# A four-layer convolution network on one core: input loads mixed with transposes, averages next to dense slots, halo copies spread out, the last halves turned sooner, and one quarter's squares paced by VectorE's sums

## The chip, the core and the metric

The kernel runs on one core of one Trainium2 chip, in one launch. The metric is the device time in microseconds; smaller is better. The engines are called TensorE (PE in the profile, its weight loads PEld), VectorE (DVE), ScalarE (ACT), GpSimd (POOL) and SyncE (SP, which here only issues DMAs). GB/s and KB are as the profile prints them.

## What is computed

The input x has the shape (1024, 16, 16, 16): batch, height, width, channel, all float32. Four layers follow each other, each adding its result to x:

```python
x = x + L0(_gn(x))   # a tensor-train matrix: three small cores, together 4096 x 4096
x = x + L1(_gn(x))   # two fixed 3x3 filters by channel, fc0 (48 -> 128), relu, fc1 (128 -> 16), masks
x = x + L2(_gn(x))   # a 3x3 convolution, 16 -> 16 channels, plus bias
x = x + L3(_gn(x))   # as L1, with weights of its own

def _gn(v, G=8, eps=1e-5):          # normalise over height, width and two channels
    g = v.reshape(B, H, W, G, C // G)
    m, s = mean(g, (1, 2, 4)), var(g, (1, 2, 4))
    return ((g - m) / sqrt(s + eps)).reshape(v.shape)
```

In L1 and L3 the sum x + d is multiplied by a mask: a place is kept where the largest of the 3 x 3 neighbours (over height and width) of channel 3 is above 0.1, in the layer's input and in d. The kernel counts the neighbours that are above it by small matmuls (pcnt). fc0 reads rows of 48 consecutive numbers of the array with its 48 channels ahead of width and height.

## The kernel before

**Tiling.** The batch is cut into two chunks of 512 columns (n = 0 and 1). A chunk of x is a tile X0 or X1 in the on-chip memory: 128 partitions, 32 lines, 512 columns. Between layers x goes through DRAM (`xf`). All matmuls are float32; each stands in the trace as two instructions.

**Stages.** The program is one sequence of stages: the first layer in five phases (up to about 1760 us), L1 on chunk 0 and on chunk 1 (to about 2270), the convolution on chunk 0 and on chunk 1 (to about 2490), L3 on chunk 0 (to about 2740) and on chunk 1 with the output (to the end). While a stage multiplies, the group norm of the next one runs beside it: VectorE sums lines (`line_sum`), TensorE averages the sums over groups by a matmul with `gm_cw` or `gm_wc` (`mean`, `mean_q`), ScalarE copies the average out (`held`), VectorE subtracts it (`each`), ScalarE or VectorE squares (`squares`), VectorE sums the squares, TensorE averages those (`var`, `var_q`), `rstd` makes the root's inverse, and VectorE scales. In `parts_cw` this goes by four quarters of eight lines.

**Order.** Every engine runs its instructions in the order in which the program writes them. `run` writes it: it goes through the stage's own steps (`main`), and after each it appends those steps of the background list whose due time, worked out from costs and a part (lo to hi) of the stage, has passed. Numbers in the background lists are pauses or costs, not waits of the machine.

```python
for i, step in enumerate(main):
    step()
    ...
    while todo and (todo[0][0] < part or i == len(main) - 1):
        todo.pop(0)[1]()
```

**First layer.** At the start chunk 0 is read by SyncE, turned by TensorE transposes (`turn`, line 866) and stored as lines in `xr` by POOL (line 881). Chunk 1 is read by POOL in eight loads of 1024 KB (line 848) during phase 0. SyncE reads `gq` (line 1040), from which `build` makes weights on TensorE (pw, line 1057); `build` takes the four banks of the tag "w", and ScalarE copies them out (line 1062). Transposes and the small matmuls `pg` of `gs` take banks by the tag "mw", which alternates between the one bank of tag "m" and the four of tag "w" (`bank`, with `either`).

**L1 and L3.** A slot is either a group of up to four matmuls of 32 rows by 128 columns each, in different row strips of the array (ph, line 1521), or a dense slot: four matmuls of 128 rows by 32 columns in different column strips (fc1, po, line 1358). `plan` gives their order; between two dense slots stand one to five ph slots, three in most places. ScalarE takes ph to hid with a relu (line 1524), VectorE takes po to u (line 1370), and GpSimd, or VectorE for the last tiles, applies mask and residual. The dense result and all averages share two banks of tag "o" (`shared[0]` is "o" in these stages, "m" in the others). Ready rows of ph have six banks. `after(n, fn)` writes fn n slots later. In the last stage the last four quads are cut into halves of 256 columns, and `turn` transposes a finished residual (ptx, line 1420) to the output's layout; with the last tile of a half, four stores of 1024 KB go out on SyncE (line 1435).

**Convolution.** Rows of output come in pairs, in seven steps: `first`, `middle` for each row, one `across`, and `last` for each; `across` takes rows of neighbours from a halo tile `hx` that ScalarE copies (line 1210), eight copies for every four rows, one popped from `pending` after each step. ScalarE also takes the results out (line 1270).

Of the kernel before, what the change touches and what calls it, by code (L numbers as in the profile page):

```python
# [103 lines left out]
def conv_preact_kernel(ctx: ExitStack, tc: tile.TileContext, a: dict, out: bass.AP):  # L104
# [585 lines left out]
    def rstd(st, rows=slice(0, P)):  # L690
# [16 lines left out]
        return [2, root, 3, (6, newton)]  # L707

    def norm_lines(X, on_act=True):
        parts = [lambda l=l: X[:, l : l + 2] for l in range(0, NL, 2)]  # L710
        s1, steps = line_sum(parts, "s1", False)
        s2, more = line_sum(squares(X, 0, NL, on_act), "s2", True, not on_act)
        st = {}

        def mean():
            st["p"] = psum([P, NB], "pmean")
            T.matmul(st["p"], gm_wc, s1["s"], start=True, stop=True)

        def var():
            st["v"] = psum([P, NB], "pvar")  # L720
            T.matmul(st["v"], gm_wc, s2["s"], start=True, stop=True)

        def keep():
            st["ve"] = work([P, NB], "n", "ve")
            V.tensor_scalar(st["ve"], st["v"], GN_EPS, None, ALU.add)

        subs = each(X, 0, NL, lambda: st["m", 0], ALU.subtract)
        steps = steps + [5, mean, 2, held(st), 2] + centred(subs, more)
        steps += [5, var, 2, keep] + rstd(st)
        return steps + by_rows(each(X, 0, NL, lambda: st["r"], ALU.mult))  # L730

    def parts_cw(X, on_act):

        st = {}
        N = defaultdict(list)
        for q in range(4):
# [4 lines left out]
            N["sums"].append(more1)  # L741
            N["sq"].append(
                centred(each(X, l0, 8, lambda q=q: st["m", q], ALU.subtract), more2)
            )
            rows = slice(32 * q, 32 * q + 32)

            def mean_q(s1=s1):
                st["p"] = psum([P, NB], "pmean")
                T.matmul(st["p"], gm_cw, s1["s"], start=True, stop=True)  # L749

# [15 lines left out]

            N["mean"].append(mean_q)
            N["var"].append(var_q)
            N["keep"].append(keep_q)
# [12 lines left out]
    def norm_cw(X, on_act):  # L782
# [6 lines left out]
        for q in (1, 2):  # L789
            steps += woven(  # L790
                sums[q + 1], (1, var[q - 1]), (3, keep[q - 1]), (3, mean[q]), (4, hold[q])
            ) + [2] + sq[q][:4]
# [233 lines left out]
    def layer_train():  # L1026
# [18 lines left out]
        def build(u):  # L1045
# [6 lines left out]
            k0 = 2 if m1 == 2 else 0  # L1052
            pw = [bank([P, 2, 16 - 4 * k0, S], "w", "pw") for _ in range(4)]
            for v in range(2):
                for r in range(4):
# [134 lines left out]
    def layer_conv(X, n, other):  # L1190
# [64 lines left out]
        def step(*fs):  # L1255
            def go():
                for f in fs:
                    f()
                if pending:
                    pending.pop(0)()  # L1260
# [24 lines left out]
    def layer_nca(X, n, l, L, xo=None):  # L1285
# [119 lines left out]
        def residual(q, w2, hf=None):  # L1405
# [7 lines left out]
            else:  # L1413
                after(8, lambda: turn(q, w2, r, hf))

# [65 lines left out]
        def step(slot):  # L1481
            def go():
# [4 lines left out]
                else:  # L1487
                    for x in slot:
                        tile_of_row(*x)
                due = [fn for n, fn in later if n <= t]  # L1490
                later[:] = [x for x in later if x[0] > t]
# [42 lines left out]
    def run(layer, us, loads, *spans, by=0.0):  # L1534
# [21 lines left out]
        for i, step in enumerate(main):  # L1556
            step()
            part = (i + 1) / len(main)
            while done < len(loads) and done < len(loads) * part / (by or 1e-9):
                loads[done]()  # L1560
                done += 1
            while todo and (todo[0][0] < part or i == len(main) - 1):
                todo.pop(0)[1]()

# [22 lines left out]
    with ExitStack() as es:  # L1587
# [32 lines left out]
            x for j in range(2) for i in range(4) for x in stat[j][i] + lines[j][4 * i : 4 * i + 4]  # L1620
        ]
        run(
            steps_of(phases[0]), 130, (),
            (late[:6] + loads[0:4] + late[6:] + loads[4:] + later + woven_in + tail + normed(0, 1) + combined(0, False), 0.0, 1.0),
        )
# [4 lines left out]
        for i in (2, 3):  # L1630
# [3 lines left out]
            )  # L1634
        nst, N = parts_cw(X0, True)
        for q in range(4):
# [23 lines left out]
    with ExitStack() as es:  # L1660
# [7 lines left out]
        run(  # L1668
            (lambda: None, main1), 108, load_cw(X0, xf[3][0]) + [put(L3)], (norm_cw(X0, True), 0.09, 1.06), by=0.07
        )  # L1670
# [37 lines left out]
```

## Time and profile before

| | us |
|---|---|
| median of three runs | 3043.31 (3041.16 to 3043.62) |
| the profiled execution | 3039.35 |
| its span in the trace | 3037.6 |

| engine | what it does most | busy us |
|---|---|---|
| TensorE | po of the first layer (line 1134), 3584 instructions | 1573.9 |
| TensorE | ph of L1 and L3 (line 1521), its two largest groups | 568.8 and 298.6 |
| ScalarE | hid (line 1524), 1040 instructions of 680 ns | 656.2 |
| VectorE | r (line 1170), 576 instructions of 684 ns | 377.9 |
| GpSimd | res and u (lines 1410, 1409), 123 each | 205.4 and 192.9 |

Such a table is read with care: busy time is a mean over stages that have different limits. The profile also gives the span in 40 slices, with the share of full speed that TensorE's clock was granted, and the trace answers for any stretch which engine was busy and which wait ended before an instruction. A wait is named after the instruction that came last by the profile, for instance "PE ph L1521 <- ACT hid L1524": a matmul of line 1521 waited for ScalarE's instruction of line 1524.

### The profile page before, as it was taken

What the parts mean: (1) busy time and instruction counts of PE and PEld (TensorE: products, weight loads), DVE (VectorE), ACT (ScalarE), POOL (GpSimd) and SP (SyncE); (2) the same over time, 40 slices, a digit from 0 to 9 for tenths busy, and PEclk for the clock granted to TensorE, in tenths of its full rate; (3) what the DMA queues carried; (4) which work ended last, traced back from release to release, by engine and by line L of the source; (5) the groups of instructions that cost most, each with busy time, mean ns of one, the idle gap of its engine ahead of it and who ended that gap; (6) DMA issues with size and microseconds to landing.
All of it is one profiled execution on the core that took longest, in us unless ns stands there. A gap on an engine that the chain in (4) does not pass through costs nothing.

```text
span 3037.6 us, 36802 instructions
## 1 busy us (share of the span) xinstructions
PE 2973.1 (98%) x13810; PEld 1245.4 (41%) x13810; DVE 1764.0 (58%) x2352; ACT 1102.7 (36%) x1822; POOL 669.9 (22%) x727
## 2 busy tenths in 40 slices
PE   7999999999999999999999999999999999999997
PEld 4444334444444444444444433333333333333333
DVE  5354337555554555544555668756977765856433
ACT  4431441000000000000101156666667656666564
POOL 2135670200000000000000015434542223442321
PEclk9999999999999999999999999999999999999998
DMA  8643664533334333332222235436337866343466
GB/s 313 232 120 99 150 152 145 166 109 109 109 109 158 115 109 109 109 102 89 88 89 94 71 130 168 137 119 204 124 122 182 188 97 207 126 129 111 134 176 208
DMA packets 251522, 418.39 MB, mean 138 GB/s; under 512 B 34869, under 2 KB 105065, under 8 KB 248273
## 3 DMA queue, kind: packets, MB, share of 16 engines
q1 hardware_dynamic: 225776, 362.53, 36.2%
q0 software_dynamic: 25376, 53.38, 8.5%
q8 instruction: 109, 1.79, 0.2%
q14 instruction: 69, 0.56, 0.1%
q10 hardware_dynamic: 192, 0.13, 0.0%
HBM read 238.58 MB, written 165.53 MB: 133 GB/s over the span
## 4 chain that ended last, share of the span: by engine, by line
PE 92%; DVE 2%; DMA 1%; issue 1%; ACT 1%; POOL 1%; SPq 0%; DVEq 0%; POOLq 0%; ACTq 0%
PE po L1134 51%; PE ph L1521 22%; PE po L1358 8%; PE po L1222 4%; PE pw L1057 3%; PE po L1231 1%; PE L_conv_pe L392 1%; PE ptin L866 1%; DVE bn L860 1%; PE ptx L1420 1%; PE pvar L753 1%; PE pr L765 0%; PE pmean L749 0%; POOL res L1410 0%; ACT hx L1210 0%
## 5 line engine op out<-in xcount | busy, mean ns | idle before, releaser
L1134 PE MATMUL po<-xn,w 128*128 128x512 f32 x3584 | 1573.9, 596 | 1.2 <-DVE xn L946 1.1
L1134 PEld LDWEIGHTS po<-xn,w 128*128 128x128 f32 x3584 | 670.3, 190 | 839.8 <-issue 820.6
L1524 ACT ACTIVATE hid<-ph,pack 128x512 f32<-128x512 f32 (+1 forms) x1040 | 656.2, 680 | 381.3 <-PE ph L1521 267.7
L1170 DVE TENSOR_TENSOR r<-r,po 128x512 f32<-128x512 f32 x576 | 377.9, 684 | 577.4 <-PE po L1134 525.0
L1409 POOL TENSOR_TENSOR u<-u,mask 128x512 f32<-128x512 f32 x123 | 192.9, 1568 | 1815.3 <-DVE mask L1403 1395.6
L1062 ACT COPY w<-pw 128x512 f32<-128x512 f32 (+1 forms) x320 | 150.6, 556 | 1209.9 <-issue 1006.3
L1521 PE MATMUL ph<-xn,wq 32*128 32x512 f32 (+1 forms) x3752 | 568.8, 600 | 0.0
L1521 PEld LDWEIGHTS ph<-xn,wq 32*128 32x128 f32 x3752 | 239.4, 184 | 268.2 <-issue 235.9
L1521 PE MATMUL ph<-xn,pack 32*128 32x512 f32 x1288 | 298.6, 624 | 4.9 <-ACT hid L1524 3.0
L1358 PE MATMUL po<-hid,pack 128*32 128x512 f32 (+1 forms) x2080 | 282.1, 602 | 0.0
L1075 DVE TENSOR_TENSOR w<-w 128x512 f32<-128x512 f32 x320 | 210.9, 686 | 88.7 <-ACT w L1062 88.6
L655 DVE TENSOR_TENSOR xn<-xn,m 128x1024 f32<-128x1024 f32 x160 | 216.0, 1380 | 47.2 <-ACT m L678 47.0
L1410 POOL TENSOR_TENSOR res<-res,u 128x512 f32<-128x512 f32 x123 | 205.4, 1670 | 9.7
L1370 DVE SCALAR_TENSOR_TENSOR u<-po,pack,xn 128x512 f32<-128x512 f32 (+1 forms) x130 | 96.3, 741 | 189.9 <-PE po L1358 185.6
L1222 PE MATMUL po<-xn,convw 128*128 128x512 f32 x368 | 167.8, 608 | 2.9 <-ACT conv L1270 2.9
L1521 PEld LDWEIGHTS ph<-xn,pack 32*128 32x128 f32 x1288 | 115.1, 185 | 104.1 <-issue 64.6
L1170 DVE TENSOR_TENSOR xn<-xn,po 128x512 f32<-128x512 f32 x96 | 64.4, 684 | 123.7 <-PE po L1134 123.3
L1358 PEld LDWEIGHTS po<-hid,pack 128*32 128x32 f32 x2080 | 43.6, 108 | 193.0 <-issue 142.3
L622 DVE TENSOR_TENSOR sq<-sq 128x1024 f32<-128x1024 f32 x78 | 109.8, 1408 | 13.3 <-ACT sq L640 12.6
L1222 PEld LDWEIGHTS po<-xn,convw 128*128 128x128 f32 x368 | 69.1, 192 | 100.3 <-issue 91.5
L404 POOL DMA_DIRECT2D L_conv_wy<-xn x160 | 89.1, 565 | 27.5 <-ACT xn L398 16.2
L1057 PE MATMUL pw<-R,gq 32*128 32x256 f32 (+1 forms) x1280 | 88.4, 381 | 3.1 <-DMA gq<-g_dram 2.9
(166 smaller groups left out, 1770.1 us busy)
## 6 DMA issues: line engine op xcount, KB each, us to landing
xf<-r SPq DMA_DIRECT2D x112, 512.0 KB, 3.8
xn<-xf SPq DMA_DIRECT2D x96, 512.0 KB, 5.1
r<-xf SPq DMA_DIRECT2D x80, 512.0 KB, 4.5
wq<-L_conv_wy SPq DMA_DIRECT2D x192, 192.0 KB, 2.7
res<-xf SPq DMA_DIRECT2D x128, 256.0 KB, 3.2
xf<-res SPq DMA_DIRECT2D x96, 256.0 KB, 2.1
res<-xr SPq DMA_DIRECT2D x256, 64.0 KB, 2.8
xf<-conv POOLq DMA_DIRECT2D x64, 256.0 KB, 5.9
```

The source lines that it names most:

```text
L655: V.tensor_tensor(part, part, m().unsqueeze(1).broadcast_to([P, 2, NB]), op)
L1057: T.matmul(pw[r][:, v], st["g", u][rows, v], st["R"][rows, p % 2, 64 * k0 : 256], start=True, stop=True,)
L1062: A.copy(w[:, k0:4, :, 32 * r : 32 * r + 32].rearrange("p k t (v o) -> p v (k t) o", v=2), pw[r],)
L1075: V.tensor_tensor(w[:, k], w[:, x], w[:, y], ALU.add if sign > 0 else ALU.subtract)
L1134: T.matmul(po, st["w", u][:, matrix, t], x, start=t == 0, stop=t == 3)
L1170: V.tensor_tensor(r[at], r[at], po, ALU.add if sign > 0 else ALU.subtract)
L1222: T.matmul(st["po", h][wh], conv["fw"][:, y], X[:, 16 * wh + h + y - 1], start=y == max(0, 1 - h), stop=y == min(2, S - h),)
L1358: T.matmul(po[32 * j : 32 * j + 32], nca["w1"][:, v], hid[j], start=v == 0, stop=v == 1)
L1409: by.tensor_tensor(u, u, st["m"][:, w2, cols(hf)], ALU.mult)
L1410: by.tensor_tensor(r, r, u, ALU.add)
L1521: T.matmul(ph, w, x, start=k == 0, stop=k == len(tiles) - 1)
L1524: A.activation(h, ph, AF.Relu, bias=nca["bt"][:, r : r + 1])
```

## The change

Eight edits, all of them in the order of the work or in the shape of small matmuls:

- `average` replaces the matmul of a mean, and of `norm_lines`'s variance. In the stages whose `shared[0]` is not "m" it writes four matmuls of 32 columns in place of one of 128.
- `mean`, `var`, `mean_q` and `var_q` are marked `beside`. `run` holds a marked step back, and with it what stands behind it in the background list, until the step just written was a dense slot (other stages' steps count as dense).
- `parts_cw` gets `paced_from`; for the first layer's last quarter, which runs as `last` in L1's first stage, subtractions come first, and then `paced`: two squares, a sum, and each further square after the sum before.
- In `norm_cw` the variance of the quarter before is written one step later; and the second convolution's `norm_cw` starts at 0.12 in place of 0.09.
- `build` sets `either[0] = 1`.
- A halo copy is popped at the steps whose number n has n % 7 even, four in seven, in place of every step.
- `turn` of a half comes 4 slots after its residual, in place of 8; whole tiles keep 8.
- In phase 0 the input loads of chunk 1 are mixed with the transposes and with `later`, one load after every two steps (`mixed_in`), in place of two rows of four.

```diff
+    def average(out, w, x):
+        if shared[0] == "m":
+            T.matmul(out, w, x, start=True, stop=True)
+            return
+
+        for c in range(0, P, 32):
+            T.matmul(out[c : c + 32], w[:, c : c + 32], x, start=True, stop=True)
...
-            T.matmul(st["p"], gm_wc, s1["s"], start=True, stop=True)
+            average(st["p"], gm_wc, s1["s"])
...
-            T.matmul(st["v"], gm_wc, s2["s"], start=True, stop=True)
+            average(st["v"], gm_wc, s2["s"])
...
+    def paced(parts, st):
+        def begin():
+            st["t"], st["q"] = parts[0](), parts[1]()
+
+        def add():
+            V.tensor_tensor(st["t"], st["t"], st["q"], ALU.add)
+
+        def last():
+            st["s"] = work([P, NB], "s", "s2s")
+            V.tensor_tensor(st["s"], st["t"][:, 0], st["t"][:, 1], ALU.add)
+
+        steps = [(2, begin), (1.2, add)]
+        for part in parts[2:]:
+            steps += [1.5, (1, lambda part=part: st.update(q=part())), (1.2, add)]
+        return steps + [(0.8, last)]
...
+            if q < paced_from:
+                N["sq"].append(centred(subs, more2))
+            else:
+                s2.clear()
+                N["sq"].append(subs + paced(squares(X, l0, 8, on_act), s2))
...
-                T.matmul(st["p"], gm_cw, s1["s"], start=True, stop=True)
+                average(st["p"], gm_cw, s1["s"])
...
-            N["mean"].append(mean_q)
-            N["var"].append(var_q)
+            N["mean"].append(beside_dense(mean_q))
+            N["var"].append(beside_dense(var_q))
...
-                sums[q + 1], (1, var[q - 1]), (3, keep[q - 1]), (3, mean[q]), (4, hold[q])
+                sums[q + 1], (2, var[q - 1]), (3, keep[q - 1]), (3, mean[q]), (4, hold[q])
...
+            either[0] = 1
...
-                if pending:
+                st["n"] = st.get("n", 0) + 1
+                if pending and st["n"] % 7 % 2 == 0:
                     pending.pop(0)()
...
-                after(8, lambda: turn(q, w2, r, hf))
+                after(8 if hf is None else 4, lambda: turn(q, w2, r, hf))
...
+                go.dense = isinstance(slot, int)
...
+                near = getattr(step, "dense", True) or i == len(main) - 1
+                if getattr(todo[0][1], "beside", False) and not near:
+                    break
                 todo.pop(0)[1]()
...
+        def mixed_in(xs, ys):
+            n = len(xs)
+            return [z for i, x in enumerate(xs) for z in (*ys[2 * i : 2 * i + 2], x)] + ys[2 * n :]
+
...
-            (late[:6] + loads[0:4] + late[6:] + loads[4:] + later + woven_in + tail + normed(0, 1) + combined(0, False), 0.0, 1.0),
+            (late[:6] + mixed_in(loads[0:4], late[6:]) + mixed_in(loads[4:], later) + woven_in + tail + normed(0, 1) + combined(0, False), 0.0, 1.0),
...
-        nst, N = parts_cw(X0, True)
+        nst, N = parts_cw(X0, True, 3)
...
-            (lambda: None, main1), 108, load_cw(X0, xf[3][0]) + [put(L3)], (norm_cw(X0, True), 0.09, 1.06), by=0.07
+            (lambda: None, main1), 108, load_cw(X0, xf[3][0]) + [put(L3)], (norm_cw(X0, True), 0.12, 1.06), by=0.07
```

## What the change was expected to do, written before it ran

> **What bounds the kernel.** TensorE does. I read three parts of the page first: busy shares, the slices, and the chain that ended last.
>
> ```profile
> PE 2973.1 (98%) x13810; PEld 1245.4 (41%) x13810; DVE 1764.0 (58%) x2352; ACT 1102.7 (36%) x1822; POOL 669.9 (22%) x727
> ...
> PE 92%; DVE 2%; DMA 1%; issue 1%; ACT 1%; POOL 1%; SPq 0%; DVEq 0%; POOLq 0%; ACTq 0%
> ```
>
> So only three things can shorten it: TensorE's waits, stretches in which its clock is lowered, and its own work; and besides, what follows its last matmul. The changed kernel multiplies no more and no less. I therefore took the list of TensorE's waits, longest first in total. It is short:
>
> ```profile
> PE ptin L866 <- ACT w L1062: 3.4, 8, 0.4
> PE ph L1521 <- ACT hid L1524: 3.0, 1, 3.0
> PE po L1222 <- ACT conv L1270: 2.9, 1, 2.9
> PE pw L1057 <- DMA gq<-g_dram: 2.9, 3, 1.4
> PE pvar L753 <- DVE s2s L630: 2.7, 1, 2.7
> ...
> PE pmean L749 <- DVE s1s L630: 2.4, 1, 2.4
> ...
> PE pmean L749 <- DVE u L1370: 1.0, 1, 1.0
> ```
>
> By the timeline they stand at 63 to 66 us (gq), 1779.9 (hid), 2345.8 (conv), 2398.6 (s1s), 2413.1 (s2s) and 2600.8 (u). Next I asked for the windows just after them. The columns are the stretch, its length, five engines' busy time, the granted clock, the DMA share and GB/s:
>
> ```profile
> 61.90:65.80 3.90, 1.43 (x7) 0.88 (x6) 0.00 (x0) 0.00 (x0) 0.00 (x0) 1.00 1.01 397
> 65.80:72.60 6.80, 6.36 (x23) 3.99 (x24) 0.69 (x1) 2.37 (x6) 0.73 (x1) 0.50 0.84 332
> 1779.30:1786.10 6.80, 6.16 (x24) 2.43 (x24) 3.18 (x4) 4.53 (x8) 0.00 (x0) 0.50 0.00 0
> 2345.90:2349.30 3.40, 3.40 (x5) 1.32 (x6) 2.58 (x3) 3.35 (x6) 2.16 (x3) 0.50 0.61 72
> 2414.20:2417.60 3.40, 3.40 (x5) 1.32 (x6) 3.37 (x4) 3.06 (x3) 3.21 (x4) 0.50 0.56 70
> 2561.00:2564.30 3.30, 3.30 (x19) 1.06 (x13) 1.51 (x2) 2.53 (x4) 3.22 (x3) 0.50 0.23 65
> ```
>
> A wait is paid twice: after it the clock is 0.50 for 3.4 or 6.8 us, in which half the work is lost (1.7 or 3.4 us).
>
> [...] The rows show 0.50 behind gaps of 2.97, 2.94 and 2.67 us, and at 2561 behind one of 1.0; the 2.39 at 2398.6 had no such window. I take the rows.
>
> **The change part by part.** Sums are against the profiled execution (3039.35 us; span 3037.6); its own distance to the median, 3043.31, I carry over unchanged.
>
> *Input loads one by one.* At 50.4 us POOL issues four 1024 KB loads in a row. SP's gq reads, issued from 51.4, land behind them at 66.2 (the chain has 13.22 us of "DMA gq<-g_dram"). In the new POOL order the loads stand between line stores, each of which waits for ScalarE's copy (stores came 2.6 us and more apart), so gq meets at most one load (1 MB at 400 GB/s: 2.6 us) and is there before 63. POOL's later four loads keep their place: nothing of POOL stands among the steps they are mixed with. Gain 2.9 wait + 3.4 clock = **6.3**; 0 if DMA is still full.
>
> *`either[0] = 1` after a build.* The next transpose takes bank m, not the w bank that ScalarE is still emptying. Seven waits of 0.44 go: 3.1. Against it, one pair of `gs` now directly follows a build, its second bank being emptied behind four w copies: about 0.7 more than the 0.75 of such a pair before. Net **2.4** (0 to 3.5).
>
> *Paced squares of the last quarter.* ScalarE's queue held three squares in a row at 1773.8; the third waited 1.77 us for the first sum to free its buffer, and four hid rows queued behind it, which TensorE then missed. Now two squares, and each next one after a sum. VectorE's sub, sub, sub, then 1.5 us of flags and u, sub, sum (from 1.22 rows) puts the first sum's end near 1777.7; the third square is reached near 1778.2 behind four 0.65 us hids, so it finds its buffer free. Gain 2.97 + 3.4, less 0.5 for a remainder: **5.9**. The 3.35 us reciprocal moves by some slots; it sits before a mask now instead of before a flags, where it cost 0.96. I count no difference, with 1.5 either way.
>
> *Even halo copies.* At 2334 to 2346 ScalarE alternates a 1.06 us square with a 1.04 us copy, one copy in every step, while a step is 1.76 us (two 0.88 us matmuls): evictions come late. Now 4 copies in 7 steps, the last five steps before `across` reads. Load in 7 steps (12.3 us) falls from about 15.6 (7 copies 7.3, squares 5.7 at one per 2.28 us pair of VectorE, four evictions 2.6) to 12.5. Gain 2.94 + 1.7 = **4.6** (2 to 5).
>
> *Second convolution's sums from 0.12, var one step later.* VectorE's sums wait for X0's loads until 2393.0 and end at 2398.6; the mean stood at 2396.2. 0.03 of 108 us is 3.2 us later: it finds its sum. The variance was reached at 2410.4 and its sum ended at 2413.0, VectorE being busy without a break from 2403.9. It now comes at 2410.4 - 2.4 + 3.2 + about 1: some 1.0 us of wait is left. Gain 2.39 + 1.7 + 1.7 = **5.8** (2 to 6.8). The stage's end has cover: VectorE was idle 11.4 us before 2477.
>
> *Averages beside dense slots, in four column strips.* It touches ten means and ten variances of the three fc stages before the last. Rows from the first:
>
> ```profile
> 1928.96 1.07 PE L1358 MATMUL po<-hid,pack 128*32 128x512 f32 x8
> 1929.96 2.86 PE L1521 MATMUL ph<-xn,wq 32*128 32x512 f32 x24
> 1932.74 0.64 PE L1358 MATMUL po<-hid,pack 128*32 128x512 f32 x4
> ...
> 1933.74 1.12 PE L749 MATMUL pmean<-s1s,gm_cw 128*128 128x512 f32 x2
> 1934.80 2.00 PE L1521 MATMUL ph<-xn,wq 32*128 32x512 f32 x16
> ```
>
> A dense slot with three ph slots takes 3.78 (1928.96 to 1932.74); with a mean beside it 4.84: +1.06. A variance in the midst of ph slots (1941.37 to 1946.34) makes it 4.97: +1.19. A strip average keeps the dense slot's shape, so I price it at 0.88 (two passes of 0.44, the 1573.9/3584 of the big layer). Saved: 0.18 for each of 7 means already beside a dense slot, 0.31 for 3 means and 7 variances amid ph: 4.4, say **4.5**. [...] The rows show po x8 from start to start in 1.00 and pmean x2 in 1.06, so eight narrow passes side by side cost no more than two wide ones; I take nothing off.
> The 0.97 at 2600.8 (two averages inside one po's life made it wait for u) goes, as averages leave that place: **1.0**.
> A new wait: twice a variance and a mean are now released at the same dense slot. Of the o banks the first po still holds one, so that mean waits for VectorE's `ve` (0.69, plus latency and what VectorE has before it), with ph slots queued behind it. 0.8 to 2.5, perhaps with half-clock: **-1.5**.
>
> *Last halves sooner.* The end is a transfer:
>
> ```profile
> 3014.00:3016.00 2.00, 2.00 (x15) 1.18 (x15) 1.28 (x4) 1.00 (x4) 0.00 (x0) 1.00 0.00 0
> 3016.00:3036.20 20.20, 2.67 (x23) 1.15 (x22) 3.09 (x9) 0.85 (x3) 0.00 (x0) 0.64 1.00 415
> ```
>
> Eight 1 MB stores fill the DMA engines from the first to the end, so only their start counts: it follows the transpose of half 0's last tile, at 3014.22. Four slots sooner, that transpose stands right behind the dense slot of 3011.98, at 3012.55; its residual is done by 3011.93. Gain **1.7** (0 if res is late by as much). Half 1's tiles are ready at 3020.3, inside half 0's ten us of transfer.
>
> Sum: 6.3 + 2.4 + 5.9 + 4.6 + 5.8 + 4.5 + 1.0 - 1.5 + 1.7 = 30.7. I take off 2.7 for waits that may turn up beside other instructions, the mask counts (pcnt) above all: **28**. Profiled about 3011; median 3043.3 - 28 = **3015**.
>
> **Rivals.**
> 1. *Waits go, half-clock windows come elsewhere.* For it: at 2561 and 2096.7 a 1.0 and a 0.4 us wait on masks sufficed. Without the 10.2 us of clock: gain 17.8, 3025.5. Against: 1838.5's equal mask wait brought none. 20%.
> 2. *Only the plan moves.* gq still lands behind a full DMA (share 1.0 at 55 to 70 us), conv2's sums are still late: loses 6.3 and 5.8, and the new waits double: gain about 14, 3029. 11%.
> 3. *Slower: gated averages starve the two o banks.* 18 releases, each a wait like 2600.8's 0.97 and a 1.7 window: 48 against the 32.2 of the gains, so 16 slower, 3059. It decides from 1.8 us a release. Against: with one exception a po's `u` is 2 us or more old where its bank is wanted. 3%.
> 4. *Nothing measurable*: gains and new waits cancel, 3043. 4%.
>
> My forecast has 62%, by itself 3009 to 3021. The range runs to rivals 1 and 2: 3009 to 3028. About 0.2%, 6 us, is what a measurement here can tell; cases 1, 2 and the forecast are beyond it: faster 0.92, same 0.05, slower 0.03.
>
> **What would show it.** Each of the six waits gone from TensorE's list, except pvar<-s2s at about 1; ptin<-w gone; clock 1.00 near 66, 1780, 2346 and 2414; DMA full from about 1.7 us before; strip averages adding about 0.9 to a dense interval; a new pmean<-ve. Wrong if those windows persist, or if new rows of 1 us appear at most averages.

## The result, and the profile after

| | before | after |
|---|---|---|
| median of four runs, us | 3043.47 (3041.16 to 3044.03) | **3021.12** (3019.68 to 3024.16) |
| ratio of the times | | **0.9929**, 95% interval 0.9912 to 0.9947 |
| profiled execution, us | 3039.35 | 3020.70 |
| its span, us | 3037.6 | 3018.9 |

Faster by 22.4 us by the medians, inside the range of the forecast (3009 to 3028), whose own value was 3015 and whose main case went by itself from 3009 to 3021. The two profiled executions differ by 18.7. Most of the rest is in the one of before, which lay 4.1 us under its median; the one of after lies 0.4 under. What follows accounts for the 18.7.

TensorE's row of the page of after: the engine is busy for nearly as long as before (2973.1) and still sets the time.

```profile
PE 2968.3 (98%) x13876; PEld 1247.0 (41%) x13876; DVE 1765.1 (58%) x2352; ACT 1102.6 (37%) x1822; POOL 669.5 (22%) x727
```

The list of TensorE's waits, of after (us in total, times, the longest):

```profile
PE ph L1562 <- DVE mask L1442: 3.2, 2, 2.6
PE po L1260 <- ACT conv L1310: 2.7, 2, 2.1
...
PE pvar L789 <- DVE s2s L630: 2.0, 3, 1.1
PE pcnt L1437 <- DVE mask L1442: 1.9, 3, 1.0
...
PE pg L554 <- ACT g L557: 1.0, 2, 0.5
PE pw L1095 <- DMA gq<-g_dram: 1.0, 3, 0.4
...
PE pmean L720 <- DVE ve L797: 0.8, 1, 0.8
```

Gone are the eight waits of transposes for `w`, the 3.0 for `hid`, the 2.4 for s1s and the 1.0 for `u`. Shorter are conv, s2s and gq. **New** are 3.2 for masks, of which 2.6 in one piece, and the forecast 0.8 for `ve`.

The windows behind and around these places, of after (stretch, length, busy time of five engines, granted clock, DMA share, GB/s):

```profile
74.40:77.80 3.40, 2.41 (x22) 1.70 (x22) 0.00 (x0) 0.68 (x3) 2.15 (x4) 1.00 1.03 422
77.80:88.00 10.20, 10.11 (x28) 4.69 (x27) 3.31 (x9) 3.05 (x9) 0.00 (x0) 0.50 1.01 418
...
1801.50:1808.30 6.80, 6.80 (x26) 2.11 (x27) 2.62 (x4) 1.95 (x3) 2.42 (x2) 0.50 0.40 120
...
2338.80:2342.20 3.40, 3.40 (x8) 1.44 (x8) 2.25 (x3) 3.35 (x5) 1.75 (x2) 1.00 0.54 65
2403.00:2406.40 3.40, 2.74 (x8) 0.70 (x10) 3.33 (x4) 2.25 (x3) 2.94 (x5) 1.00 0.39 46
2545.60:2549.00 3.40, 3.40 (x18) 1.50 (x16) 3.00 (x4) 0.62 (x2) 2.66 (x2) 0.50 0.20 79
```

The clock is whole again behind the convolutions' waits (2338.8 and 2403.0). But the start's lowered stretch has only moved and grown, from 6.8 us at 65.8 to 10.2 at 77.8, and the one behind `hid` at 1779.3 has become one of the same length behind a mask at 1801.5. Between 60 us and the last stores, the clock was lowered for 27.3 us before and for 20.5 after. A stretch at 0.50 costs about half its length: eight matmuls of the first convolution took 3.70 us at full clock in after (2338.80), and 5.40 with the loads in rows, across 3.4 us of half clock (2337.82). So of 10.2 us that the forecast took from the clock, half of 6.8 came: 3.4. The other 15.3 of the 18.7 are waits and work.

By stretch, each counted from one mark in the trace to the next:

| stretch of the span | before | after | change | forecast for it |
|---|---|---|---|---|
| start to the fold of the first weights (`L_conv_pe`) | 314.7 | 311.8 | -2.9 | -8.7 |
| fold to L1's first ph | 1445.9 | 1445.8 | -0.1 | 0 |
| L1, both chunks | 516.2 | 513.0 | -3.2 | |
| both convolutions | 216.3 | 208.7 | -7.6 | -10.4 |
| L3's first ph to the first ptx | 289.8 | 286.7 | -3.1 | |
| first ptx to the end | 254.7 | 252.9 | -1.8 | -1.7 |

For L1 and L3's middle the forecast was -9.9: 5.9 for the paced squares, 4.0 net for averages. They gave -6.3.

### The profile page after: what moved, and what is told of

Read it like the earlier page. It is cut to its first block, busy times and chain, and to the rows that moved or that the text cites. A ratio compares the mean times of both kernels' runs of the same rounds, so it can differ in the third digit from the quotient of the medians.

```text
span 3018.9 us, 36939 instructions
## 1 busy us (share of the span) xinstructions
PE 2968.3 (98%) x13876; PEld 1247.0 (41%) x13876; DVE 1765.1 (58%) x2352; ACT 1102.6 (37%) x1822; POOL 669.5 (22%) x727
## 4 chain that ended last, share of the span: by engine, by line
PE 90%; issue 2%; DVE 2%; DMA 2%; POOL 1%; ACT 1%; SPq 0%; POOLq 0%; DVEq 0%; ACTq 0%
PE po L1172 51%; PE ph L1562 21%; PE po L1398 8%; PE po L1260 3%; PE pw L1095 3%; PE L_conv_pe L392 1%; PE ptin L902 1%; PE po L1269 1%; DMA xn<-xf 1%; PE ptx L1460 1%; POOL res L1450 1%; POOL u L1449 1%; DVE sq L622 1%; PE pr L801 0%; DMA xn<-in_x_dram 0%
## 5 line engine op out<-in xcount | busy, mean ns | idle before, releaser
L655 DVE TENSOR_TENSOR xn<-xn,m 128x1024 f32<-128x1024 f32 x160 | 216.3, 1383 | 35.5 <-ACT m L678 35.3
L622 DVE TENSOR_TENSOR sq<-sq 128x1024 f32<-128x1024 f32 x75 | 106.2, 1416 | 11.1 <-ACT sq L640 10.4
```

Of the source, the lines that this page charges most:

```text
L655: V.tensor_tensor(part, part, m().unsqueeze(1).broadcast_to([P, 2, NB]), op)
```

## The experiments

Two theories. **A**: each edit does what the sum said, and what is missing is two named waits that took the place of removed ones: gq of the next unit of weights, amid the loads that are now spread out, and a mask behind the long reciprocal. **B**: the edits matter little one by one, and the clock decides, dropping somewhere whatever is removed. Every experiment below is one edit or a pair of edits, taken out of the changed kernel, put into the one before, or mended. Each is timed beside the kernel before on the same chip. The kernel before had medians of 3039.37 (23 runs), 3040.10 (44) and 3041.26 (7 runs) in the three groups of runs, so ratios are compared across groups, and times only inside one.

| kernel | median, us | before, us | ratio | 95% interval |
|---|---|---|---|---|
| loads mixed, alone | 3041.88 | 3039.37 | 1.0009 | 1.0002 to 1.0015 |
| changed, loads in rows as before | 3020.62 | 3041.26 | 0.9931 | 0.9915 to 0.9948 |
| changed, loads on SyncE's queue | 3018.93 | 3039.37 | 0.9932 | 0.9916 to 0.9949 |
| changed, not paced | 3019.83 | 3039.37 | 0.9935 | 0.9920 to 0.9950 |
| changed, reciprocal in pieces | 3015.57 | 3039.37 | 0.9922 | 0.9907 to 0.9937 |
| strips alone | 3037.91 | 3040.10 | 0.9994 | 0.9985 to 1.0002 |
| beside dense slots alone | 3036.78 | 3040.10 | 0.9989 | 0.9982 to 0.9996 |
| even copies and sooner halves alone | 3037.32 | 3040.10 | 0.9991 | 0.9982 to 0.9999 |
| bank choice and later sums alone | 3030.39 | 3040.10 | 0.9969 | 0.9959 to 0.9979 |
| changed, three repairs | 3009.77 | 3041.26 | 0.9897 | 0.9882 to 0.9912 |

### The input loads

**Alone**, in the kernel before:

```diff
-            (late[:6] + loads[0:4] + late[6:] + loads[4:] + later + woven_in + ...
+            (late[:6] + mixed_in(loads[0:4], late[6:]) + mixed_in(loads[4:], later) + woven_in + ...
```

> The kernel before with the mixed input loads alone. Theory A (the loads only move the wait for gq: POOL's last four still go out in a row while the DMA engines are full, so the next unit's gq is late and TensorE's clock falls there): no wait for gq near 63 us, one of about 1 us in total near 75 to 78, a half-clock window of 6.8 to 10.2 us after it, and the big matmuls of phase 1 start within 1.5 us of the kernel before. Rival B (the gq wait of the changed kernel came with the new bank choice, which makes TensorE run ahead): no wait for gq at all, 5 to 6 us gained by 150 us.

Measured: slower, 1.0009, and the fold comes at 320.6 instead of 314.7. Theory A had the direction; the size is far beyond what it expected (a wait of about 1 us, phase 1 within 1.5 us of the kernel before). One window of this kernel says where:

```profile
90.00:95.00 5.00, 1.13 (x13) 1.14 (x15) 0.00 (x0) 0.00 (x0) 0.00 (x0) 0.87 1.02 404
```

TensorE works 1.1 of 5 us and every other engine is still; the DMA share is full. Its wait for gq is 4.5 us in one piece (before: 2.9 in three), and 13.7 us of half clock follow. 1.6 more wait and half of 6.9 more window make 5.0 of the 5.9; the transposes' waits for `w`, 4.4 us instead of 3.4, are about the rest.

**The other way round**, the changed kernel with the loads in two rows of four as before:

```diff
-            (late[:6] + mixed_in(loads[0:4], late[6:]) + mixed_in(loads[4:], later) + woven_in + ...
+            (late[:6] + loads[0:4] + late[6:] + loads[4:] + later + woven_in + ...
```

> The changed kernel with the input loads in two rows of four again, as before the change, all other edits kept. Theory A (mixing the loads on POOL only moves the wait, and the gain of the start is the bank choice's): gq waits of about 2.7 us in total at 62 to 66 with a half-clock window, as in the run with the bank choice alone, none near 76, and the mark where phase 1 folds the weights lies within 2 us of the changed kernel's 311.8. Rival B (mixing is worth 5 us or more once the banks are right): the mark at 316 or later.

0.9931 beside 0.9929, and the fold at 311.0 beside 311.8. The edit is worth nothing in the changed kernel and costs time in the one before. The timelines of after give the reason, first GpSimd's queue, then SyncE's (start, us, instruction, count):

```profile
73.66 0.72 POOL L917 DMA_DIRECT2D xr<-lines  x1 [2.08 <-ACT lines L915]
74.39 1.64 POOL L884 DMA_DIRECT2D xn<-in_x_dram  x3
```

```profile
62.83 4.54 SPq L1076 DMA_DIRECT2D gq<-g_dram  x4
```

The gq issued from 53.0 is in time now, as forecast. But the first four loads go out one by one between 54 and 68 us, among line stores of 512 KB, and four more at 74 to 77. The gq of the *next* unit is issued in four parts of 32 KB from 62.8 on, into this traffic. Its last parts take up to 10.4 us to land and TensorE gets the last at 76.6, while the DMA share is 1.01 or more from 70 us on. Three short waits (1.0 in all) and the 10.2 us at half clock behind them (5.1) cost 6.1, if all of that stretch is put down to them; those of before cost 6.3.

**On SyncE's queue**, where gq is issued too, so that the program's order separates them:

```diff
-        loads, stat, lines, tail, more = input_steps(1, tag, G)
+        loads, stat, lines, tail, more = input_steps(1, tag, nc.sync)
```

> The changed kernel with the eight input loads of chunk 1 issued by SP in place of POOL. SP's queue stands in the program's order and waits for ScalarE's results, so the loads are truly spread over the phase. Theory A (gq is late because the loads leave in rows, not because of the bytes as a whole): DMA share below 0.95 in most stretches of 60 to 90 us, no wait for gq, no half-clock window at 78, and 4 to 6 us gained on the changed kernel. Rival B (the bytes of the phase fill the DMA engines whatever the order, and on SP the gq reads now also stand behind the loads): waits for gq of 1 us or more, equal or slower time.

The fold comes at 307.4, 4.4 us sooner than in after (the kernels without pacing and with the reciprocal in pieces start with the same code as after and fold at 310.7 and 310.8, so 3.3 to 4.4), and no wait for gq is left. The windows of this kernel at the same place:

```profile
70.00:75.00 5.00, 4.83 (x36) 3.21 (x34) 0.05 (x1) 2.83 (x8) 0.72 (x1) 1.00 0.87 336
75.00:80.00 5.00, 4.75 (x21) 2.45 (x22) 3.26 (x9) 1.87 (x6) 0.00 (x0) 0.70 0.51 198
```

From 70 us on the DMA engines have air (from 65 to 70 their share is still 1.02). Four loads have been issued by 61.6, when the next unit's gq goes out, and none follows it until 77.6; in after, two follow within 5 us. A lowered stretch of 6.8 us remains at 77.0 although no wait for gq stands before it, so not all of after's 10.2 us can be put down to gq; the cause of the rest is open. The 4 to 6 us that theory A expected are seen at the fold alone: the whole time has a ratio of 0.9932 beside 0.9929 of the changed kernel, with intervals of about 5 us to either side, which neither shows the gain nor excludes it. The edit changes the queue and with it when a load may start; which of the two does it was not tried apart.

### The paced squares and the reciprocal

**Not paced**, the rest of the change kept:

```diff
-        nst, N = parts_cw(X0, True, 3)
+        nst, N = parts_cw(X0, True)
```

> The changed kernel without the pacing of the last quarter's squares, all other edits kept. Theory A (pacing is worth about 6 us by itself, which the mask's wait took back): the 3.0 us wait for hid near 1777 comes back with a half-clock window, the mask's wait near 1801 is below 1 us, and the time is within 2 us of the changed kernel's. Rival B (the mean that now follows the dense slot already brings the squares forward, so that pacing adds nothing): no wait for hid above 1 us. Rival C (both waits are there): 5 to 7 us slower than the changed kernel.

0.9935 beside 0.9929: no difference that can be told, as theory A expected. In TensorE's list of this kernel the wait for `hid` is back, and the mask's 2.6 is not there:

```profile
PE ph L1562 <- ACT hid L1565: 3.0, 1, 3.0
...
PE pcnt L1437 <- DVE flags L1406: 1.0, 1, 1.0
...
PE ph L1562 <- DVE mask L1442: 0.3, 1, 0.3
```

ScalarE's rows explain what pacing did. First without it, then in after (in brackets the idle time before, and who ended it):

```profile
1771.22 1.06 ACT L640 ACTIVATE sq<-xn 128x1024 f32<-128x1024 f32 x1 [0.53 <-DVE xn L655]
1774.05 1.06 ACT L640 ACTIVATE sq<-xn 128x1024 f32<-128x1024 f32 x1 [1.77 <-DVE sq L622]
1775.01 2.40 ACT L1565 ACTIVATE hid<-ph,pack 128x512 f32<-128x512 f32 x4
```

```profile
1770.69 1.99 ACT L640 ACTIVATE sq<-xn 128x1024 f32<-128x1024 f32 x2
1772.58 2.41 ACT L1565 ACTIVATE hid<-ph,pack 128x512 f32<-128x512 f32 x4
1774.86 1.08 ACT L640 ACTIVATE sq<-xn 128x1024 f32<-128x1024 f32 x1
```

The third square no longer stands and waits 1.77 us in front of four `hid`. TensorE's 2.97 us for `hid` is gone, as forecast. What came instead is in VectorE's rows of after:

```profile
1793.58 0.75 DVE L1410 SCALAR_TENSOR_TENSOR u<-po,pack,xn 128x512 f32<-128x512 f32 x1
1794.36 3.35 DVE L701 RECIPROCAL r<-t 32x512 f32<-32x512 f32 x1
...
1799.64 0.69 DVE L705 TENSOR_TENSOR r<-r,t 32x512 f32<-32x512 f32 x1
...
1800.70 0.69 DVE L1442 TENSOR_SCALAR mask<-pcnt 128x512 bf16<-128x512 f32 x1
```

and TensorE's row for the next matmul:

```profile
1801.45 2.03 PE L1562 MATMUL ph<-xn,pack 32*128 32x512 f32 x2 [2.57 <-DVE mask L1442]
```

The count (pcnt) was multiplied at 1796.3. VectorE reads it at 1800.7, behind the reciprocal of 3.35 us, four refining operations and a flags, 6.3 us without a gap. A count takes one of the six banks of ph; it stays full until then, and the next ph slot needs it.

**The reciprocal in two pieces of 256 columns**, with room between them and the refining operations one by one:

```diff
+        if apart:
+            return [2, root, 2, (1.6, inverse(0)), 4, (1.6, inverse(1)), 4] + [
+                x for k in range(4) for x in ((0.7, refine(k)), 0)
+            ]
...
-    last = alone(N, 3) + rstd(nst, slice(96, 128)) + [3] + scaled(N, [3])
+    last = alone(N, 3) + rstd(nst, slice(96, 128), True) + [3] + scaled(N, [3])
...
-            layer_nca(X0, 0, 1, L1), 250, load_cw(X1, xf[1][1]), (last, 0.0, 0.18),
+            layer_nca(X0, 0, 1, L1), 250, load_cw(X1, xf[1][1]), (last, 0.0, 0.205),
```

> The changed kernel with one thing more: in the last quarter of the first layer's norm, the root's inverse is written in six pieces (two reciprocals of 256 columns, four small steps) with pauses between them, in place of one step of 5.8 us. Theory A (the paced squares did remove the wait for hid, and the 2.6 us wait of a ph matmul for the mask at 1801, with its half-clock window of 6.8 us, comes from the mask standing behind the whole inverse): that wait falls below 0.5 us, the window is gone, and the kernel gains 5 to 6.5 us on the changed one. Rival B (the mask is late because VectorE has too much before it in this stretch, wherever the inverse stands): a wait of over 1.5 us stays near 1795 to 1810 and the time is within 2 us of the changed kernel's.

Against the kernel without pacing, in the same group: 3015.57 (3014.91 to 3018.89) to 3019.83 (3019.29 to 3021.37), 4.3 us less and the ranges do not meet (the changed kernel itself was not in this group; the forecast was 5 to 6.5 less than that one). From L1's first ph to the same mean later in the stage it takes 148.4 us, in after 153.6 and without pacing 153.0. VectorE's rows of this kernel:

```profile
1788.61 0.69 DVE L1470 SCALAR_TENSOR_TENSOR mask<-pcnt,mask 128x512 bf16<-128x512 f32 x1
1789.34 1.75 DVE L712 RECIPROCAL r<-t 32x256 f32<-32x256 f32 x1
1791.49 0.76 DVE L1433 TENSOR_SCALAR flags<-po,pack 32x512 bf16<-32x512 f32 x1 [0.40 <-PE po L1425]
```

A piece of 1.75 us ends before the next flags are wanted. The wait and its lowered stretch are gone: at 1801.5 to 1808.3 this kernel has clock 1.00. (A shorter one, 3.4 us at 1829.9, stands behind a mask that waits behind sums, and a matmul `pr` waits 0.7 for the last refinement.) So the pacing took its wait away and was worth something only with this repair. The repair without the pacing was not run; without pacing the trace has 1.0 us of wait behind the reciprocal, for flags, and no more than about that would be expected of it there.

### The averages

**In strips**, not held back (kernel before with `average`):

```diff
-            T.matmul(st["p"], gm_wc, s1["s"], start=True, stop=True)
+            average(st["p"], gm_wc, s1["s"])
```

> The kernel before with the averages of L1's and L3's stages in four column strips alone; where they stand is unchanged. Theory A (what a narrow average saves is the change of the array's shape, and that is saved only beside a dense slot): the interval between two dense slots that holds a mean amid ph slots stays within 0.1 us of 1.06 to 1.19 over the plain one; only means already beside a dense slot (7 of 10) lose about 0.15 each; together 1 us. Rival B (four strips run at once and are cheaper anywhere): all means cost 0.9, 2 to 3 us gained. Rival C (every strip pays its own overhead): 1 us or more lost.

**Held back to a dense slot**, not in strips (kernel before with `beside`):

```diff
+        mean, var = beside_dense(mean), beside_dense(var)
...
-            N["mean"].append(mean_q)
-            N["var"].append(var_q)
+            N["mean"].append(beside_dense(mean_q))
+            N["var"].append(beside_dense(var_q))
...
+                near = getattr(step, "dense", True) or i == len(main) - 1
+                if getattr(todo[0][1], "beside", False) and not near:
+                    break
```

> The kernel before with the averages held back until a dense slot alone; means stay one matmul of 128 columns. Theory A: the variances, which are 32 columns wide already, cost about 0.9 in place of 1.19 us (seven amid ph slots: 2 us gained), the means beside a dense slot 1.06, and a mean that is released together with a variance waits about 0.8 us for ve; net 1 to 2 us gained, all of it in the three fc stages. Rival B (holding back delays VectorE's chain): new waits of 1 us or more at ph or po in these stages, nothing gained.

Ratios 0.9994 and 0.9989: the first can't be told from nothing, the second is 3.3 us. Both are better read from the length of a dense interval, from one dense slot to the next with three ph slots between (3.78 us without an average), in four kernels:

| average in the interval | amid ph slots | beside the dense slot |
|---|---|---|
| mean of 128 columns | 5.05 (before) | 4.84 (before, and held back alone) |
| mean in four strips | 4.99 (strips alone) | **4.64** (strips alone, and after) |
| variance of one strip | 4.97 (before) | **4.64** (after) |

In after, such a row is

```profile
1930.11 1.07 PE L1398 MATMUL po<-hid,pack 128*32 128x512 f32 x8
1930.99 1.04 PE L720 MATMUL pmean<-s1s,gm_cw 128*32 128x512 f32 x8
1931.96 2.00 PE L1562 MATMUL ph<-xn,wq 32*128 32x512 f32 x16
...
1934.75 1.07 PE L1398 MATMUL po<-hid,pack 128*32 128x512 f32 x8
```

from 1930.11 to 1934.75. The dense slot and the average lie against each other (1930.99 is 0.88 after 1930.11; with the mean of 128 columns it was 1.00). Strips pay only beside a dense slot; amid ph slots they give 0.06. Beside a dense slot an average costs 0.86 instead of 1.06 to 1.27: with the forecast's counts 7 x 0.20 + 3 x 0.41 + 7 x 0.33 = 4.9.

### Halo copies and halves; bank choice and the second convolution's sums

The edits of the convolution and the end, in two pairs whose places in the trace do not overlap:

```diff
-                if pending:
+                st["n"] = st.get("n", 0) + 1
+                if pending and st["n"] % 7 % 2 == 0:
...
-                after(8, lambda: turn(q, w2, r, hf))
+                after(8 if hf is None else 4, lambda: turn(q, w2, r, hf))
```

> The kernel before with two edits that lie 650 us apart, so that the profile tells them apart: even halo copies, and the last halves turned 4 slots after their residual. Theory A: in the first convolution the wait of po for ScalarE's eviction falls only from 2.9 to about 2.1 us, because by then the eviction stands behind squares that wait for VectorE, not behind copies; without the half-clock window if the shorter wait does not trip it. The last stores start 1.7 us sooner after the first transposed output tile, and the end with them. Rival B (ScalarE's load alone made the wait): below 0.5 us. Rival C (the end is bound by something else than the stores): the distance from the first ptx matmul to the end is unchanged at 254.7 us.

TensorE's wait for conv goes from 2.9 to 2.1, as in after, and the end is 1.9 us shorter (252.8). The half-clock stretch behind the wait stays here (3.4 us at 2349.7). In after it is gone; the last section shows how the wait lies there. The rest of the wait has another cause than the copies' number. ScalarE's rows of after:

```profile
2333.64 1.06 ACT L640 ACTIVATE sq<-xn 128x1024 f32<-128x1024 f32 x1
2335.91 1.06 ACT L640 ACTIVATE sq<-xn 128x1024 f32<-128x1024 f32 x1 [1.21 <-DVE xn L655]
2336.99 1.04 ACT L1248 COPY hx<-xn 32x1024 f32<-32x1024 f32 x1
2338.06 1.26 ACT L1310 ACTIVATE conv<-po,b 128x512 f32<-128x512 f32 x2
```

Before the late eviction, ScalarE stands still for 1.21 us: a square waits for VectorE's subtraction, and a copy and the eviction stand behind it. ScalarE has the time; what is wrong is the order.

```diff
-                sums[q + 1], (1, var[q - 1]), (3, keep[q - 1]), (3, mean[q]), (4, hold[q])
+                sums[q + 1], (2, var[q - 1]), (3, keep[q - 1]), (3, mean[q]), (4, hold[q])
...
+            either[0] = 1
...
-            ... load_cw(X0, xf[3][0]) + [put(L3)], (norm_cw(X0, True), 0.09, 1.06), by=0.07
+            ... load_cw(X0, xf[3][0]) + [put(L3)], (norm_cw(X0, True), 0.12, 1.06), by=0.07
```

> The kernel before with two edits that lie 2200 us apart: the bank choice after a build, and the second convolution's norm from 0.12 with each variance one step later. Theory A: the seven waits of 0.44 us of transposes for w are gone (3 us), one wait of pg grows; the gq wait of the kernel before stays at 2 to 5 us in total, since TensorE runs ahead; in the second convolution the waits for s1s (2.4) and s2s (2.7) fall to 0 and about 1 us and the half-clock window near 2414 is gone: from the first convolution matmul to L3's first ph 4 to 6 us less than 216.3. Rival B (the sums only wait later, at the next quarters): the variances of quarters 1 to 3 wait 2 us or more in total.

The largest pair, 0.9969. The fold comes at 310.4, 4.3 us sooner, with gq as late as before; the convolutions take 211.0, 5.3 less. In its list of waits `ptin <- w` and `pmean <- s1s` are gone, and what is left of the sums is

```profile
PE pvar L753 <- DVE s2s L630: 1.8, 3, 0.8
```

Before it was one wait of 2.7. Two of the three, 1.0 us together, are new and stand at later quarters, so rival B was right in a small part.

Taken together, the single edits (1 - ratio: 0.0006, 0.0011, 0.0009, 0.0031) make 0.0057, or 17 us, beside 0.0069 (0.0052 to 0.0085) for the changed kernel with the loads left in rows: they add up, within the intervals.

### Three repairs together

The loads on SyncE's queue, the reciprocal in pieces, and in `norm_lines` a pause among the squares and at most one average for each dense slot:

```diff
+        sq = centred(subs, more)
+        if on_act:
+            sq = sq[:4] + [3] + sq[4:]
+        steps = steps + [2 if on_act else 5, mean, 2, held(st), 2] + sq
...
+            apart = False
...
-                if getattr(todo[0][1], "beside", False) and not near:
-                    break
+                if getattr(todo[0][1], "beside", False):
+                    if not near or apart:
+                        break
+                    apart = i < len(main) - 1
```

> The changed kernel with four further edits, each in a stretch of its own: the inverse in pieces and the input loads on SP as in the two kernels before; in the first convolution's norm the mean is written 3 us sooner and a pause of 3 us stands after the first square's subtraction (theory: the eviction's 2.1 us wait comes from squares written sooner than VectorE can subtract, so that ScalarE holds them in front of evictions; it falls below 0.5 us, and the stretch from the first convolution matmul to L3's first ph from 208.7 to about 206.5; rival: the wait stays at 2 us, since VectorE's rate of 2.27 us a pair and not its start is what lags); and at most one average is released at a dense slot (theory: the waits of pmean for ve, 0.78 and 0.13, are gone). Together with 5.2 and 4.3 us from the first two: 3010 to 3013 us.

3009.77 (3008.61 to 3011.78) in one group with the changed kernel whose loads stand in rows, 3020.62 (3020.08 to 3022.51): 10.9 us less, ratio to the kernel before 0.9897 (0.9882 to 0.9912), so it is faster than the kernel before and than the changed one with loads in rows (the changed kernel itself was not in this group; the two have ratios of 0.9929 and 0.9931). The first convolution's wait, the wait for `ve` and the 2.6 for a mask are gone. Its list has these left, for the places spoken of here:

```profile
PE pcnt L1467 <- DVE mask L1472: 2.5, 3, 1.1
...
PE pvar L819 <- DVE s2s L630: 2.3, 3, 1.1
...
PE po L1290 <- ACT conv L1340: 1.7, 2, 0.9
...
PE pw L1125 <- DMA gq<-g_dram: 1.2, 1, 1.2
```

The last is new beside the kernel with the loads on SyncE's queue: it ends at 100.3 us, at a later unit's gq. The start's wait is smaller and has moved once more.

The convolutions take 208.2 us, only 0.5 less than in after, where 2.2 had been forecast: 2.1 us of wait left the first, and 1.4 came back in the second's evictions (0.80 and 0.88, in after one of 0.60) and variances.

## Where the prediction was right, and where not

| step | forecast, us | measured, us | from |
|---|---|---|---|
| loads one by one | 6.3 | 0 | loads in rows; alone it costs 5.9 at the fold |
| bank choice | 2.4 | 3.7 to 4.3 | fold of the kernel with loads in rows, and of bank choice alone |
| paced squares | 5.9 | -0.5 | L1's first ph to the last mask count of its first tiles: 77.9 before, 78.5 after |
| halo copies | 4.6 | 0.8, and 1.7 by luck | first convolution's wait; its lowered stretch, which came back in two other kernels with the same wait |
| second convolution's sums | 5.8 | 5.1 | second convolution |
| averages, with the wait for `ve` | 4.0 | 5.1 | what is left of L1 and L3, less 1.7 for a stretch at 2096.7 whose clock is now whole |
| last halves | 1.7 | 1.8 | first ptx to the end |

**Wrong: the loads.** The step that failed reads "so gq meets at most one load ... and is there before 63 ... POOL's later four loads keep their place". It is true of one read of gq, and the forecast stopped there. Loads that are spread out do not become fewer: the next unit's gq, issued from 62.8 on, is there at 76.6 only. Nor did the later four keep their place: they were issued from 80.1 us on before and from 74.4 on after. The forecast had priced "0 if DMA is still full" and put it into the second rival. That rival's first half came true.

**Wrong: the reciprocal.** "The 3.35 us reciprocal moves by some slots; it sits before a mask now instead of before a flags, where it cost 0.96. I count no difference, with 1.5 either way". The order had been read correctly, the price had not: before a mask it cost 2.57 and 6.8 us at half clock, 6.0 in all and about as much as the pacing had saved. (A further 0.59 for a mask at 1821.8 stands behind two scalings of VectorE, not behind the reciprocal.) A mask has a bank of TensorE's behind it. What stood in the queue behind the reciprocal should have been counted through, four refining operations among it, as I did for ScalarE's squares.

**Half right: the copies.** The load (12.5 us in 12.3) was judged right: ScalarE even stands idle. The step took a queue's load for its order. The square in front of the eviction waits for VectorE, whatever the number of copies. With the mean written sooner and a pause among the squares, in the kernel with repairs, the wait goes; which of the two does it was not tried apart. The forecast also counted 1.7 for the clock behind this wait. That came in after, but by luck: with the loads in rows the wait is as long (2.12) and the lowered stretch is there.

**Right:** the second convolution (no wait for the mean, and 1.08 for the variance where 1.0 was forecast), the strip average (0.88 forecast, 0.86 found), the new wait of 0.8 for `ve`, and the end. Taking nothing off for the larger number of matmuls was right too: from start to start the eight narrow passes of the row above take 0.97 us (1930.99 to 1931.96), two wide ones took 1.06 (1933.74 to 1934.80, before). The bank choice was priced too low: the extra wait of pg did not come, and pg's waits for g became shorter (2.2 us before, 1.4 with loads in rows and with bank choice alone).

**The rivals.** The profiled gain, 18.7, is close to what the first rival gave (17.8: waits go, half-clock windows come elsewhere), and yet it is not how it went. 17.1 of the 20.5 us at half clock in after follow two waits that have names, `gq` with the small weight matmuls around it and a mask. The mask's stretch goes when its wait does; of the start's, 6.8 stayed when the wait for gq was gone. Theory A holds for the edits, and for the mask it is shown. B keeps the rest of the start's stretch and the small windows below. The 2.7 us kept back for waits beside other instructions was, with hindsight, the right kind of entry and half the size.

That the time lies in the range is no proof of the sum. The loads and the paced squares were 12.2 of its 30.7 us and gave -0.5; the range was wide enough for that because it reached to the rivals, and the account covers 18.7 of the 22.4 us: the other 3.7 are the distance of the two profiled executions to their medians.

## What to carry to other kernels

When a transfer is moved out of the way of one read, follow the *next* reads of that queue too: what is moved has to pass somewhere, and with full DMA engines the next read came in time here only where the program's own order kept the loads away from it (on SyncE's queue: no wait for gq, DMA share 0.87 at 70 to 75 us; in after 1.0 us of waits at 1.01 or more). When an instruction is moved to another place in an in-order queue (without pacing, four `hid` stood behind one square that waited 1.77 us), look up who waits for what stands behind it, and count its followers with it. A long one next to something that holds a bank of the bounding engine was best cut here: in one piece of 3.35 us it cost a wait of 2.57, in two of 1.75, with its followers spread out, that wait was gone. And an engine that is lightly loaded can still be late, as ScalarE's eviction was by 2.1 us behind 1.21 of its own idle time: read the idle time in front of its late instruction, and who ended it, before taking work off it.

## What the runs showed of the clock

I had expected a lowered stretch behind a long enough wait. The traces of before and after show a grid. In each of the two, all lowered stretches after 60 us start whole multiples of 3.413 us apart, to about a thousandth of a step, however the waits lie. In before, those at 1779.30 and 2096.74 are 317.44 us apart, 93 steps; in after, those at 1801.52 and 2545.63 are 744.11 apart, 218 steps. In the convolutions the stretches go with TensorE's idle time within one cell of this grid, and not with the length of the wait. The first convolution's wait is the same in two kernels, 2.11 us in after and 2.12 with the loads in rows. Three cells of the kernel with loads in rows:

```profile
2335.60:2339.00 3.40, 1.28 (x4) 0.67 (x4) 3.40 (x4) 3.33 (x5) 0.94 (x2) 1.00 0.00 0
2339.00:2342.40 3.40, 3.40 (x5) 1.35 (x4) 1.60 (x2) 3.38 (x5) 1.85 (x3) 0.50 0.91 120
2342.40:2345.80 3.40, 3.40 (x12) 0.86 (x11) 1.92 (x2) 2.90 (x4) 0.72 (x1) 1.00 1.04 145
```

and of after:

```profile
2334.00:2337.40 3.40, 2.69 (x7) 0.91 (x5) 3.40 (x4) 2.16 (x3) 0.00 (x0) 1.00 0.01 2
2337.40:2340.80 3.40, 2.00 (x5) 1.04 (x6) 2.96 (x3) 3.32 (x5) 1.75 (x2) 1.00 0.20 10
2340.80:2344.20 3.40, 3.40 (x12) 0.78 (x11) 1.82 (x2) 3.37 (x5) 1.75 (x2) 1.00 1.01 149
```

In the first the wait lies in one cell (TensorE busy 1.28 of 3.40), and the next has clock 0.50. In the second a border splits it into 0.7 and 1.4, and the clock stays at 1.00.

In the traces of before and after (first 60 us and last stores left out) five cells at full clock had 2.29 us of idle time or more, and each was followed by half clock: in before 2.48 at 62.39, 2.33 at 1775.89, 2.94 at 2342.50 and 2.29 at 2410.77, in after 2.57 at 1798.11. In the convolutions of these two the other cells had up to 1.52 us, and none was followed by it. The two waits of before's second convolution lie so: a border splits the 2.39 us at 2398.6 into cells with 0.87 and 1.52 us of idle time, and no lowered stretch follows; the 2.67 at 2413.1 leaves 2.29 in one cell, and 3.4 us at 0.50 follow. So waits of equal length, as the 2.11 and 2.12 above, can differ in what follows them.

The same kernel before took 3032.66 to 3044.89 us in two groups, and its mean clock goes with that in part: in the group of 44 runs those of clock 0.989 took 3041.23 to 3044.43, those of 0.993 3035.80 to 3038.87.

Left open: outside the convolutions, cells with less idle time were followed by half clock in some places (in before 0.75 us at 2093.33 and 1.32 at 2557.54, in after 0.99 at 74.38 and 1.14 at 2542.22) and in others were not (in before 0.96 at 1803.19 and 1.19 at 2830.61, in after 1.20 at 2811.87). What sets these apart was not tried. Nor were the mask waits of about 1 us at 2545 and the wait of 1.2 for the first `ptx`, which all kernels here have.
